# A recurrent four-way convolution scan: one transfer queue in program order, scalings placed under the column scans, larger hand-overs and a re-cut last pass

## The chip, the cores and the metric

The kernel runs on one core of a Trainium2 chip. The metric is the device time of one execution in microseconds (us). A core has a matrix engine (PE, with its weight loads shown as PEld), a vector engine (DVE), a scalar engine (ACT), GpSimd (POOL) and SyncE (SP). Each runs its own instructions in a fixed order and waits at an instruction until what it needs is there. SP and ACT also issue transfers (DMAs), in that same order.

## The reference

The input has 32 images of 48 channels, 64 rows and 128 columns, in f32. Two layers of this are computed, each with weights of its own:

```
def step(w, b):
    def f(carry, inp):
        nxt = inp + _conv1d(carry, w, b)      # 5 taps, 48 -> 48 channels
        return (nxt, nxt)
    return f
... D: scan over the rows downwards, U: over the rows of D upwards (same weights)
... R: scan over the columns of U to the right, L: over those of R to the left
x = x + _L0_conv_ref(_gn(x), ...)             # _gn: mean and variance over 3 channels x 64 x 128
x = x + _L1_conv_ref(_gn(x), ...)
```

Each row needs the row before it, each column the column before it: 63 + 63 + 127 + 127 dependent steps a layer.

## The kernel before

The images go in four groups of eight (GB), so there are eight passes: (layer 0, group 0) is pass 0, (layer 1, group 0) pass 4. Names in the profile carry layer and group: `row_12d` is the PSUM tile of a down step in layer 1, group 2; `col_03l` that of a left step in layer 0, group 3.

A pass is a down scan and an up scan over rows (`row_step`: nine matmuls and three additions on DVE, the ends at L462), a hand-over to a layout by columns, and a right and a left scan (`col_step`: two independent halves of four images, three matmuls and one addition on DVE at L483 each). The layouts `rows` and `cols` lie in one SBUF tile, `arena`; `rows` reaches past its first part into the region of `cols`. A hand-over of some rows (`hand_over`, L372) is 20 DMAs from SBUF to SBUF: ten pieces of channels for odd rows and ten for even ones. It is done for eight rows at a time, and for the last rows in pieces that end at rows 4, 2 and 0 (`SPLITS`); of rows below 8 the odd ones are issued by ACT, everything else by SP.

Around the scans stands other work:

- `prepare` reads a group of the input (L319), permutes it on POOL (L331), and stores it in DRAM as `xin` (L334). For group 0 this comes before everything else, with the statistics by DVE.
- `fetch` loads rows of `xin` (layer 0) or `mid` (layer 1) for a pass by ten DMAs from ACT's queue (L352), and ACT scales them (L356, 24 instructions).
- `input_moments` and `result_moments` read a group again for the group norm (L280, L292); ACT sums (L195) and squares (L204). A tile of a result takes eight plus eight ACT instructions, of an input one plus one.
- `scaling` turns the moments into scale and offset: a chain over DVE, PE, DVE, PE, DVE, ACT (the square root, `std`, L255) and DVE.
- `drain` and `residual` add a finished pass to its input while the next one runs (POOL, L382 or L388), storing `mid` or the output. `last_residual` does so for the last pass under its left scan, by quarters of the columns (L416 loads, L424 additions, L432 stores).

The program writes this side work between scan steps, and a scheduler that models the engines then sets the order on each of them. The DMAs go through eight lanes that SP and ACT share: each waits for the one eight places before it.

Of the kernel before, what the change touches and what calls it, by code (L numbers as in the profile page):

```python
# [34 lines left out]
C = 48  # L35
ODD = 64
P = ODD + C
TAPS = 5
# [11 lines left out]
RB = 8  # L50
DOWN, RIGHT, LEFT = range(3)

LOADS = tuple(slice(a, b) for a, b in ((0, 4), (4, 12), (12, 20))) + tuple(
    slice(a, min(a + 8, 64)) for a in range(20, 64, 8)
)
EARLY = 3
SPLITS = {4: 8, 2: 4, 0: 2}
# [28 lines left out]
def kernel(  # L86
# [35 lines left out]
    wd = const([FULL, len(PRODUCTS), FULL], "wd")  # L122
# [7 lines left out]
    nats = [const([P, CH, PAIR], f"nat{i}") for i in range(2)]  # L130
    perms = [const([P, CH, PAIR], f"perm{i}") for i in range(2)]
# [3 lines left out]
    ]  # L135

# [4 lines left out]


    nc.gpsimd.memset(arena[32:64, H * ROW + 7 * CH * PAIR :], 0.0)
    for t in nats + perms:
        nc.vector.memset(t[32:64], 0.0)
    nc.vector.memset(wd, 0.0)
# [3 lines left out]
    nc.scalar.dma_start(mask_sb, mask)  # L150
    nc.scalar.dma_start(bc, bias)
    for e, c0, c1, o, p0 in PIECES:
        nc.scalar.dma_start(bd[p0 : p0 + c1 - c0, :, o], bias[c0:c1, :, DOWN])
        nc.scalar.dma_start(maskp[:, o, p0 : p0 + c1 - c0], mask[:, c0:c1])

    def load_row_weights(layer: int, eng):

        for eo, a0, a1, o, m0 in PIECES:
            for k in range(TAPS):
                shift, ei = divmod(eo + k - TAPS // 2, E8)  # L160
                d, si = divmod(k, 2)
                for e, c0, c1, i, p0 in PIECES:
                    if e == ei:
                        eng.dma_start(
                            wd[
                                p0 : p0 + c1 - c0,
                                PRODUCTS.index((i, o, shift)),
                                m0 : m0 + a1 - a0,
                            ],
                            w[SIDES[si], layer, DOWN, d, SIDES[0]][c0:c1, a0:a1],  # L170
                        )

    def load_col_weights(layer: int, eng):
        eng.dma_start(wc, w[:, layer, RIGHT : LEFT + 1])
# [5 lines left out]
    class Moments:  # L180


        def __init__(self, parts: int, n: int, key: str):
            self.T, self.n, self.key = parts, n, key
            mean = stat_tile(GB * parts, f"mean{parts}", key)
            dev2 = stat_tile(GB * parts, f"dev2{parts}", key)
            self.mean = mean.rearrange("p (b t) -> p b t", t=parts)
            self.dev2 = dev2.rearrange("p (b t) -> p b t", t=parts)

    def collect(mo, t: int, views, key: str):  # L190


        bs = slice(min(views), max(views) + 1)
        for b, view in views.items():
            nc.scalar.activation(  # L195
                view, view, AF.Identity, scale=sides, accum_out=mo.mean[:, b, t : t + 1]
            )
        neg = stat_tile(GB, "neg", key)
        nc.gpsimd.tensor_scalar(neg[:, bs], mo.mean[:, bs, t], -1.0 / mo.n, None, ALU.mult)  # L199
        nc.gpsimd.tensor_scalar(  # L200
            mo.mean[:, bs, t], mo.mean[:, bs, t], 1.0 / mo.n, None, ALU.mult
        )
        for b, view in views.items():
            nc.scalar.activation(  # L204
                view,
                view,
                AF.Square,
                bias=neg[:, b : b + 1],
                accum_out=mo.dev2[:, b, t : t + 1],
            )  # L210

    def scaling(mo):

        key, T = mo.key, mo.T
        ps = ps_stat.tile([FULL, NG + 1, 2 * GB], F32, tag="ps_stat", name=f"ps_{key}")
        pair = stat_tile(2 * GB, "pair", key)
        if T > 1:
            total = stat_tile(GB, "total", key)
            nc.vector.tensor_reduce(total, mo.mean, mybir.AxisListType.X, ALU.add)
            nc.vector.tensor_scalar(pair[:, 0:GB], total, 1.0 / T, None, ALU.mult)  # L220
        else:
            nc.vector.tensor_copy(pair[:, 0:GB], mo.mean[:, :, 0])  # L222
        nc.tensor.matmul(ps[0:P, NG, 0:GB], mask_sb, pair[:, 0:GB], start=True, stop=True)  # L223
        mean_p = stat_tile(GB, "mean_p", key)
        nc.vector.tensor_copy(mean_p, ps[0:P, NG, 0:GB])
        dev = stat_tile(GB * T, f"dev{T}", key).rearrange("p (b t) -> p b t", t=T)
        nc.vector.tensor_tensor(
            dev, mo.mean, mean_p.unsqueeze(2).to_broadcast([P, GB, T]), ALU.subtract
        )
        sq = stat_tile(GB * T, f"sq{T}", key).rearrange("p (b t) -> p b t", t=T)  # L230
        nc.vector.tensor_tensor(sq, dev, dev, ALU.mult)
        all_sq = stat_tile(GB * T, f"all{T}", key).rearrange("p (b t) -> p b t", t=T)
        nc.vector.scalar_tensor_tensor(all_sq, mo.dev2, 1.0 / mo.n, sq, ALU.mult, ALU.add)
        if T > 1:
            total2 = stat_tile(GB, "total2", key)
            nc.vector.tensor_reduce(total2, all_sq, mybir.AxisListType.X, ALU.add)
            nc.vector.tensor_scalar(pair[:, GB:], total2, 1.0 / T, None, ALU.mult)
        else:
            nc.vector.tensor_copy(pair[:, GB:], all_sq[:, :, 0])
        for o in range(NG):  # L240
            nc.tensor.matmul(ps[:, o], maskp[:, o], pair, start=True, stop=True)
# [7 lines left out]
        var = small("var")  # L249
        nc.vector.tensor_scalar(var, ps[:, 0:NG, GB:], GN_EPS, None, ALU.add)  # L250
        mean = small("mean")
        nc.vector.tensor_copy(mean, ps[:, 0:NG, 0:GB])

        std = small("std")
        nc.scalar.activation(std, var, AF.Sqrt)  # L255
        r0 = small("r0")
        nc.vector.reciprocal(r0, std)
        t0 = small("t0")
        nc.vector.tensor_tensor(t0, var, r0, ALU.mult)
        t1 = small("t1")  # L260
        nc.vector.tensor_tensor(t1, t0, r0, ALU.mult)
        t2 = small("t2")
        nc.vector.tensor_scalar(t2, t1, -0.5, 1.5, ALU.mult, ALU.add)
        scale = small("scale", 2 * NGRP)
        nc.vector.tensor_tensor(scale, r0, t2, ALU.mult)
        offset = small("offset", 2 * NGRP)
        nc.vector.scalar_tensor_tensor(offset, mean, -1.0, scale, ALU.mult, ALU.mult)
        return scale, offset

    def input_moments(g: int):  # L270

        parts, n = 2, H * W // 4
        mo = Moments(parts, n, f"x{g}")
        coeffs[0, g] = mo
        for b in range(GB):
            for t in range(parts):
                tile_ = perms[t].rearrange("p r n -> p (r n)")
                flat = x[g * GB + b].rearrange("c (s t h) w -> s t c (h w)", s=2, t=parts)
                for s in range(2):
                    nc.sync.dma_start(tile_[SIDES[s]], flat[s, t])  # L280
                collect(mo, t, {b: tile_}, f"x{g}_{b}{t}")
                yield
        coeffs[0, g] = scaling(mo)
# [362 lines left out]
```

## Time and the profile before

| what | value |
|---|---|
| median of 3 runs | 5947.53 us (5943.52 to 5948.58) |
| the profiled execution | 5961.04 us, its span 5959.3 |
| PE busy | 4860.6 us, 82% of the span |
| DVE, ACT, POOL busy | 2548.1, 1812.3, 1087.5 us |
| moved by DMA | 599.97 MB, mean 101 GB/s |
| granted PE clock, mean | 0.922 |

PE's share is an average: in a column scan with nothing beside it PE is busy all the time, elsewhere it waits. So the question for each stage is what it waits for. The queue of waits names the tile or engine that came last ("PE col_12r L476 <- DMA arena<-arena: 52.7, 1, 52.7": in all 52.7 us, once, at longest 52.7). Windows give busy time per engine in a stretch, and after the clock the busy share of the DMA engines and GB/s. An issue row ("SPq L372 ... x170") gives the start, the time that the queue took for that many DMAs, and the line.

### The profile page before, as it was taken

Reading aid. Unit: us, or ns where it says so; the run is one execution under the profiler, and the core shown is the slowest. Engines: PE = TensorE matmul, PEld = TensorE weight load, DVE = VectorE, ACT = ScalarE, POOL = GpSimd, SP = SyncE. Lnnn points to the kernel's source line nnn. Section 1 sums busy time; section 2 is a strip of 40 time slices with the busy share of each in tenths; the row PEclk is TensorE's granted clock in tenths of the full one; section 3 lists DMA queues with packets and bytes.
Section 4 is the critical chain, followed back from the end, with each engine's and each line's share of the span. In section 5 each row is a group of like instructions: output and inputs, shape, how many; then the busy total and the mean of one; then the engine's idle time right before and its main releaser. Section 6 shows DMA issues by size and latency. Waiting matters only on the chain. (4 is left out here: it accounts for less than half of the span.)

```text
span 5959.3 us, 105466 instructions
## 1 busy us (share of the span) xinstructions
PE 4860.6 (82%) x42592; PEld 4846.2 (81%) x42592; DVE 2548.1 (43%) x7387; ACT 1812.3 (30%) x3977; POOL 1087.5 (18%) x640
## 2 busy tenths in 40 slices
PE   0496999889996998795997969869698799986990
PEld 0496999889996998795997969869698799986990
DVE  3343554445443553342543535335354345433550
ACT  0451234024220396077050840308603020220000
POOL 3101303121221303000030001510015100350043
PEclk9998999999998999897998989989799899998995
DMA  7665838477465738442184412754117510463045
GB/s 149 118 114 108 174 64 184 106 155 151 98 158 109 167 66 192 111 84 54 22 184 109 84 19 44 149 122 83 30 34 151 121 37 1 95 129 89 1 69 92
DMA packets 847369, 599.97 MB, mean 101 GB/s; under 512 B 267584, under 2 KB 783680, under 8 KB 842272
## 3 DMA queue, kind: packets, MB, share of 16 engines
q1 hardware_dynamic: 603840, 483.73, 39.7%
q10 hardware_dynamic: 243040, 109.49, 9.5%
q8 instruction: 335, 5.49, 0.4%
q14 instruction: 154, 1.26, 0.1%
HBM read 341.31 MB, written 150.99 MB: 83 GB/s over the span
## 5 line engine op out<-in xcount | busy, mean ns | idle before, releaser
L356 ACT ACTIVATE arena<-arena,offset_m,scale_m 128x128 f32<-128x128 f32 (+1 forms) x864 | 425.6, 584 | 1243.6 <-DMA arena<-mid 895.1
L356 ACT ACTIVATE arena<-arena,offset_x,scale_x 128x128 f32<-128x128 f32 (+1 forms) x864 | 422.4, 590 | 901.2 <-DMA arena<-xin 738.6
L195 ACT ACTIVATE perm<-perm,sides 112x256 f32<-112x256 f32 (+1 forms) x560 | 476.2, 858 | 577.1 <-DMA perm<-in_x 192.4
L388 POOL TENSOR_TENSOR perm<-arena,nat 112x1024 f32<-112x1024 f32 x96 | 360.8, 3785 | 1154.8 <-DVE arena L483 459.7
L382 POOL TENSOR_TENSOR nat<-arena,nat 112x2048 f32<-112x2048 f32 x64 | 289.2, 4533 | 671.5 <-DMA nat<-xin 353.9
L204 ACT ACTIVATE perm<-perm,neg_m 112x256 f32<-112x256 f32 x512 | 381.0, 752 | 13.7 <-POOL neg_m L199 13.7
L331 POOL COPY perm<-nat 112x1024 f32<-112x1024 f32 x100 | 200.0, 2034 | 646.7 <-DMA nat<-in_x 599.8
L199 POOL TENSOR_SCALAR neg_m<-mean_m 112x8 f32<-112x8 f32 x64 | 15.1, 236 | 1250.1 <-ACT perm L195 1250.1
L424 POOL TENSOR_TENSOR perm<-arena,nat 112x256 f32<-112x256 f32 x108 | 114.4, 1067 | 485.4 <-DVE arena L483 328.1
L223 PE MATMUL ps_x<-pair_x,mask_sb 112*112 112x8 f32 x8 | 1.6, 276 | 237.2 <-DVE pair_x L222 221.4
L223 PEld LDWEIGHTS ps_x<-pair_x,mask_sb 112*112 112x112 f32 x8 | 1.5, 231 | 237.4 <-DVE pair_x L222 221.4
L476 PE MATMUL col_10r<-arena,wc 112*112 112x128 f32 x508 | 106.3, 292 | 97.3 <-DVE arena L483 50.9
L454 PE MATMUL row_13d<-arena,wd 128*128 128x128 f32 x1134 | 141.7, 291 | 30.0 <-DVE arena L462 30.0
L454 PEld LDWEIGHTS row_13d<-arena,wd 128*128 128x128 f32 x1134 | 139.1, 206 | 32.5 <-DVE arena L462 32.5
L454 PE MATMUL row_11d<-arena,wd 128*128 128x128 f32 x1134 | 137.7, 286 | 29.9 <-DVE arena L462 29.9
L454 PEld LDWEIGHTS row_11d<-arena,wd 128*128 128x128 f32 x1134 | 135.2, 201 | 32.0 <-DVE arena L462 32.0
L454 PE MATMUL row_12d<-arena,wd 128*128 128x128 f32 x1134 | 138.6, 287 | 27.7 <-DVE arena L462 27.7
L454 PEld LDWEIGHTS row_12d<-arena,wd 128*128 128x128 f32 x1134 | 136.0, 202 | 29.8 <-DVE arena L462 29.8
L476 PE MATMUL col_03l<-arena,wc 112*112 112x128 f32 x508 | 105.5, 290 | 67.2 <-DVE arena L483 67.2
L476 PE MATMUL col_11l<-arena,wc 112*112 112x128 f32 x508 | 105.4, 290 | 59.2 <-DVE arena L483 59.2
L454 PE MATMUL row_03d<-arena,wd 128*128 128x128 f32 x1134 | 137.1, 286 | 18.2 <-DVE arena L462 18.2
L454 PEld LDWEIGHTS row_03d<-arena,wd 128*128 128x128 f32 x1134 | 135.2, 201 | 20.0 <-DVE arena L462 19.8
(228 smaller groups left out, 13956.7 us busy)
## 6 DMA issues: line engine op xcount, KB each, us to landing
arena<-arena SPq DMA_DIRECT2D x672, 96.0 KB, 2.5
xin<-perm SPq DMA_DIRECT2D x128, 384.0 KB, 5.2
nat<-xin SPq DMA_DIRECT2D x128, 384.0 KB, 8.6
mid<-nat SPq DMA_DIRECT2D x128, 384.0 KB, 5.1
perm<-mid SPq DMA_DIRECT2D x128, 384.0 KB, 6.3
nat<-in_x SPq DMA_DIRECT2D x100, 384.0 KB, 8.0
perm<-in_x SPq DMA_DIRECT2D x96, 384.0 KB, 6.3
nat<-mid SPq DMA_DIRECT2D x96, 384.0 KB, 6.9
```

Of the source, the lines that this page charges most:

```text
L195: nc.scalar.activation(view, view, AF.Identity, scale=sides, accum_out=mo.mean[:, b, t : t + 1])
L199: nc.gpsimd.tensor_scalar(neg[:, bs], mo.mean[:, bs, t], -1.0 / mo.n, None, ALU.mult)
L204: nc.scalar.activation(view, view, AF.Square, bias=neg[:, b : b + 1], accum_out=mo.dev2[:, b, t : t + 1],)
L223: nc.tensor.matmul(ps[0:P, NG, 0:GB], mask_sb, pair[:, 0:GB], start=True, stop=True)
L331: nc.gpsimd.tensor_copy(perm5[:, r], nat[:, r])
L356: nc.scalar.activation(view[:, o, b], view[:, o, b], AF.Identity, bias=offset[:, o, b : b + 1], scale=scale[:, o, b : b + 1],)
L382: nc.gpsimd.tensor_tensor(nat, res, nat, ALU.add)
L388: nc.gpsimd.tensor_tensor(perm[:, t].rearrange("p (b k e) -> p b k e", b=GB, k=NK), cols[:, q + t].rearrange("p e k b -> p b k e"), nat[:, ...
L424: eng.tensor_tensor(perm[:, t].rearrange("p (b k e) -> p b k e", b=GB, k=kn), cols[:, q + t, :, ks].rearrange("p e k b -> p b k e"), nat[: ...
L454: nc.tensor.matmul(ps[o][:, a:b], wd[:, n], prev[:, i, a + s * GB : b + s * GB], start=seen[o] == 1, stop=seen[o] == left[o],)
L476: nc.tensor.matmul(ps, wt[:, 1], prev, start=True, stop=False)
```

## The change

All bulk transfers go through one helper, `dma()`, on SP, and keep the order in which the program writes them (before, the scheduler could move them). ACT issues only the first weights and half of the last stores.

- Hand-overs are 16, 16, 16, 8 and 8 rows (`HANDS`), odd rows first: 100 DMAs a pass where there were 200.
- `fetch` is split into `load_rows` and `scale_rows`; `residual` has its loads ahead of time (`load_residual`); four staging tiles replace two pairs.
- Moments are staged in `spare`, three tiles in the region of rows 0 to 15, which no one uses during right and left scans. So all moments move there: those of the next input first, then those of the last pass's result (`all_moments`). `neg` is computed on ACT instead of POOL.
- `scaling` is a generator with a few instructions between steps, each told to follow the newest scan step (`issue_after`). For the input it is started at right step 80, for results in an up scan from row 60 on, two passes after the pass that made that result.
- For group 0 all input loads come first, and half of the permuting goes to ACT.
- `drain` is spread over the down scan alone and completed at the start of the up scan.
- `last_residual` loads 96 KB at a time (128 loads instead of 256; 256 stores as before), parts 3, 2, 1, 0 as the left scan sets them free, from step 96 on.
- Row weights are built from five tap copies in DRAM, by 10 wide DMAs.

```diff
-SPLITS = {4: 8, 2: 4, 0: 2}
+HANDS = {48: 64, 32: 48, 16: 32, 8: 16, 0: 8}
...
+    def dma(dst, src):
+        tc.keep_in_program_order(nc.sync.dma_start(dst, src))
...
-        nc.gpsimd.tensor_scalar(neg[:, bs], mo.mean[:, bs, t], -1.0 / mo.n, None, ALU.mult)
-        nc.gpsimd.tensor_scalar(
-            mo.mean[:, bs, t], mo.mean[:, bs, t], 1.0 / mo.n, None, ALU.mult
-        )
+        nc.scalar.mul(mo.neg[:, bs, t], mo.sum[:, bs, t], -1.0 / mo.n)
...
+    spare = [arena[0:P, i * CH * PAIR : (i + 1) * CH * PAIR] for i in range(3)]
...
     def hand_over(h0: int, h1: int):
-        for r in range(2):
-            eng = nc.scalar if r and h1 <= RB else nc.sync
+        for r in (1, 0):
...
-            if h % RB == 0 and h:
-                hand_over(h, h + RB)
-            elif h in SPLITS:
-                hand_over(h, SPLITS[h])
+            if h in HANDS:
+                hand_over(h, HANDS[h])
...
+    def all_moments(n: int):
+        if n + 1 < NGRP:
+            yield from input_moments(passes[n + 1][1])
+        if 0 < n <= NGRP:
+            yield from result_moments(n - 1)
...
+            if stage_name == "down" and i % 7 in (1, 4):
+                advance("drain")
+            if stage_name == "up":
+                complete("drain")
+                if i == 60 and 2 <= n <= NGRP + 1:
+                    side["scaling"] = scaling(moments[1, n - 2], 1, n - 2)
+                if i % 2:
+                    advance("scaling")
+            if stage_name == "right":
...
+                if i % 6 == 2:
+                    advance("prepare")
+                if i % 4 == 2 and i < 66 and n + 1 < NGRP:
+                    advance("moments")
+                elif i % 8 == 2:
+                    advance("moments")
+                if i == 80 and n + 1 < NGRP:
+                    side["scaling"] = scaling(moments[nxt], *nxt)
+                if i % 4 == 0:
+                    advance("scaling")
+            if stage_name == "left":
...
+                if i % 8 == 2:
+                    advance("moments")
+                if nxt and i in (50, 40, 25):
+                    complete("moments")
+                    load_rows(*nxt, (50, 40, 25).index(i))
+                    scale_rows(*nxt, (50, 40, 25).index(i))
+                if nxt and i == 15:
+                    for j in range(4 - 2 * layer):
+                        load_residual(n, j)
+                if not nxt and i <= 96 and i % 8 == 0:
+                    advance("last")
```

How this falls on the engines is not in the diff, since the scheduler has a part in it. First SP at the end of the first pass's up scan. Before, the last rows' hand-over stands there in pieces of two rows (48x2x128 and, by sides, 48x128), followed by the next group's restaging (`xin` stores, `in_x` loads):

```order
L372 DMA arena<-arena 16x128
L372 DMA arena<-arena 48x128 x2
L372 DMA arena<-arena 16x128
L372 DMA arena<-arena 32x128
L372 DMA arena<-arena 48x128 x4
L372 DMA arena<-arena 32x128
L372 DMA arena<-arena 16x128
L372 DMA arena<-arena 48x128 x2
L372 DMA arena<-arena 16x128
L372 DMA arena<-arena 32x128
L372 DMA arena<-arena 48x128 x2
L334 DMA xin_86<-perm_83 48x2x1024 x2
```

After, it holds groups of 8 rows (four of one side in a DMA), both sides on SP; the next group's input loads follow:

```order
L147 DMA arena<-arena 16x4x128
L147 DMA arena<-arena 48x4x128 x2
L147 DMA arena<-arena 16x4x128
L147 DMA arena<-arena 32x4x128
L147 DMA arena<-arena 48x4x128 x4
L147 DMA arena<-arena 32x4x128
L147 DMA arena<-arena 16x4x128
L147 DMA arena<-arena 48x4x128 x2
L147 DMA arena<-arena 16x4x128
L147 DMA arena<-arena 32x4x128
L147 DMA arena<-arena 48x4x128 x2
L147 DMA stage<-in_x 48x8x256 x4
```

So the pieces of the end became fewer and four times as high, and ACT's half came to SP. Second, ACT in pass 1 (layer 0, group 1). Before, the square root of the next group's scaling (`std_x`) stands behind the last rows of a load, in the down scan, ahead of ACT's hand-over DMAs:

```order
L352 DMA arena<-xin_86 32x4x128
L352 DMA arena<-xin_86 16x4x128
L352 DMA arena<-xin_86 48x4x128 x2
L352 DMA arena<-xin_86 32x4x128
L352 DMA arena<-xin_86 48x4x128 x2
L356 ACTIVATE arena<-arena,offset_x_2744,scale_x_2742 128x4x16 x24
L255 ACTIVATE std_x_7997<-var_x_7993 128x24
L372 DMA arena<-arena 48x128
L372 DMA arena<-arena 16x128
```

After, it stands behind the last tile of the next input's moments (`sum_x`, `neg_x`, `dev_x`), and ahead of all 16 tiles of a result's moments (`sum_m`, `neg_m`, `dev_m`), behind which come the scales for the next pass (L411):

```order
L196 ACTIVATE arena,sum_x_7873<-arena,sides 112x2048
L199 ACTIVATE neg_x_7874<-sum_x_7873 112x1
L201 ACTIVATE arena,dev_x_7875<-arena,neg_x_7874 112x2048
L273 ACTIVATE std_x_9144<-var_x_9140 128x24
L196 ACTIVATE arena,sum_m_8656<-arena,sides 112x256 x8
L199 ACTIVATE neg_m_8657<-sum_m_8656 112x8
L201 ACTIVATE arena,dev_m_8658<-arena,neg_m_8657 112x256 x8
L196 ACTIVATE arena,sum_m_8656<-arena,sides 112x256 x8
```

What moved is that the result's moments now share the pass with the input's and stand behind `std_x`. Third, DVE at that `std_x`: before, `var_x`, which it needs, is computed among the additions of the down scan's step 36 in pass 1:

```order
L225 COPY mean_p_x_7979<-ps_x_7973 112x8
L227 TENSOR_TENSOR dev_x_7981<-mean_x_5774,mean_p_x_7979 112x16
L231 TENSOR_TENSOR sq_x_7983<-dev_x_7981 112x16
L233 SCALAR_TENSOR_TENSOR all_x_7985<-dev_x_5775,sq_x_7983 112x16
L236 TENSOR_REDUCE total_x_7987<-all_x_7985 112x8
L237 TENSOR_SCALAR pair_x_7974<-total_x_7987 112x8
L250 TENSOR_SCALAR var_x_7993<-ps_x_7973 128x24
L252 COPY mean_x_7995<-ps_x_7973 128x24
L462 SCALAR_TENSOR_TENSOR arena<-row_01d_6577,bd,arena 128x128
```

After, it stands among the additions of the left scan of that pass, behind both halves of step 60 (counted down from 126; one row is one half):

```order
L563 SCALAR_TENSOR_TENSOR arena<-col_01l_10287,bc,arena 112x32x4
L245 TENSOR_TENSOR dev_x_8968<-dev_x_8968 112x16
L563 SCALAR_TENSOR_TENSOR arena<-col_01l_10292,bc,arena 112x32x4
L248 SCALAR_TENSOR_TENSOR dev_x_8968<-dev_x_7875,dev_x_8968 112x16
L252 TENSOR_REDUCE total_x_9035<-dev_x_8968 112x8
L563 SCALAR_TENSOR_TENSOR arena<-col_01l_10297,bc,arena 112x32x4
L253 TENSOR_SCALAR pair_x_8855<-total_x_9035 112x8
L563 SCALAR_TENSOR_TENSOR arena<-col_01l_10302,bc,arena 112x32x4
L268 TENSOR_SCALAR var_x_9140<-ps_x_8918 128x24
L270 COPY mean_x_9142<-ps_x_8918 128x24
L563 SCALAR_TENSOR_TENSOR arena<-col_01l_10307,bc,arena 112x32x4
L278 RECIPROCAL r_x_9245<-std_x_9144 128x24
```

So this chain went from the down scan to the middle of the left scan, with scan steps between its parts.

More of the change, by code (lines that the diff above doesn't have):

```diff
@@ L135 @@
     ]
+    taps = [
+        dram.tile([C, TAPS, C], F32, tag=f"taps{i}", name=f"taps{i}") for i in range(2)
+    ]
+    passes = [(layer, g) for layer in range(2) for g in range(NGRP)]
+    coeffs, moments, mark = {}, {}, {}
     rows = arena[:, 0 : H * ROW].rearrange("p (h o n) -> p h o n", h=H, o=NG)
@@ L227, in scaling @@
[L227 to L234, printed above, removed]
+            nc.vector.tensor_reduce(total, mo.sum, mybir.AxisListType.X, ALU.add)
```

579 lines of the change are left out of this document (307 added, 272 removed).

## The prediction

> **What bounds the kernel now.** I read the page's head first, then one undisturbed window, the queue of what PE waited for, windows over the row scans, and the issue rows of SP and ACT.
>
> ```profile
> span 5959.3 us, 105466 instructions
> ...
> PE 4860.6 (82%) x42592; PEld 4846.2 (81%) x42592; DVE 2548.1 (43%) x7387; ACT 1812.3 (30%) x3977; POOL 1087.5 (18%) x640
> ...
> 4800.00:5100.00 300.00, 300.00 (x2688) 300.00 (x2687) 157.19 (x448) 25.98 (x52) 0.00 (x0) 1.00 0.02 5
> ```
>
> The window 4800:5100 is a column scan with nothing in its way: PE is busy for all of its 300 us, at clock 1.00, one matmul record each 300/2688 = 111.6 ns. The 42592 records at that pace are 4754 us. A row step has 18 records (2.01 us), 63 of them make a down or an up scan of 126.6; a column step has 12 (1.34 us), 127 make 170 us, so right and left together are 341. The change leaves these matmuls alone, so 4754 is the floor and 5959 - 4754 = 1205 us can be won. Here is what PE waited for:
>
> ```profile
> PE ps_x L223 <- DVE pair_x L222: 221.4, 1, 221.4
> PE col_03l L476 <- DVE arena L483: 67.2, 1, 67.2
> PE col_11l L476 <- DVE arena L483: 59.2, 1, 59.2
> PE col_12r L476 <- DMA arena<-arena: 52.7, 1, 52.7
> PE col_10r L476 <- DVE arena L483: 50.9, 1, 50.9
> PE col_11r L476 <- DMA arena<-arena: 50.9, 1, 50.9
> PE col_13r L476 <- DMA arena<-arena: 48.3, 1, 48.3
> PE col_03r L476 <- DMA arena<-arena: 47.2, 1, 47.2
> PE col_10r L476 <- DMA arena<-arena: 46.4, 1, 46.4
> PE col_01r L476 <- DMA arena<-arena: 45.1, 1, 45.1
> PE col_02r L476 <- DMA arena<-arena: 44.9, 1, 44.9
> PE col_00r L476 <- DMA arena<-arena: 35.0, 1, 35.0
> ...
> PE ps_x L223 <- DVE pair_x L220: 15.9, 1, 15.9
> ...
> DVE total_m L219 <- POOL mean_m L200: 177.8, 3, 67.3
> ```
>
> Eight waits for the hand-over, one at each start of a right scan, make 371 us, with the 16 us of a late scaling beside the first. Three stalls inside column scans make 177; they are one thing, DVE standing at L219 for moments that are not ready (177.8 in three). The start and the row scans are seen in windows (PE busy, clock, DMA share and GB/s at the end of a row; the two sums are over passes 1 to 3, and over 4 to 7):
>
> ```profile
> 0.00:230.00 230.00, 2.35 (x9) 2.15 (x10) 70.38 (x167) 5.14 (x12) 76.78 (x44) 1.00 0.85 165
> 230.00:368.00 138.00, 132.07 (x1135) 131.30 (x1135) 60.53 (x188) 123.37 (x229) 2.11 (x10) 0.99 0.31 58
> ...
> sum 447.38, PE 402.26 PEld 399.36 DVE 199.72 ACT 247.76 POOL 164.16; mean PE 134.09 PEld 133.12 DVE 66.57 ACT 82.59 POOL 54.72
> ...
> sum 659.42, PE 555.13 PEld 547.00 DVE 286.14 ACT 304.35 POOL 312.81; mean PE 138.78 PEld 136.75 DVE 71.54 ACT 76.09 POOL 78.20
> ...
> 5810.00:5959.00 149.00, 0.45 (x5) 0.25 (x3) 12.99 (x22) 0.00 (x0) 50.88 (x49) 0.51 0.60 92
> ```
>
> The first down scan ends at 368, 241 over its 126.6. The others exceed it by 447 - 380 = 67 in layer 0 and 659 - 506 = 153 in layer 1. The tail is 149. Together: 4754 + 241 + 387 + 177 + 220 + 149 = 5928; the 31 left go to short waits and slow clock after long ones, and I keep 16.
>
> **The change, part by part.**
>
> *Hand-over.* It is 200 DMAs a pass now and 100 after, all on SP, the odd rows' side first and no splits of 4, 2 and 2 rows at the end.
>
> ```profile
> 1070.91 145.89 SPq L372 DMA_DIRECT2D arena<-arena  x170
> 1161.05 26.09 ACTq L372 DMA_DIRECT2D arena<-arena  x30
> ...
> arena<-arena SPq DMA_DIRECT2D x672, 96.0 KB, 2.5
> ```
>
> SP issues from 1071 to 1217 without a break while the up scan ends at 1167: the queue is 50 us late, and that is the wait. One issue is 0.63 us near its best, landing 2.5. With 20 DMAs (12.6 us) per 16 rows (32 us), and the last two groups of 8 rows 16 us apart, SP is idle when the last group comes. Its ten odd-side DMAs are ready 2 us before the end and are out 4.3 us after it; the first columns' pieces of the other side follow, two issues and a landing: about 9 us, if the first matmul waits for these alone; if for all ten of that side, 13. Eight make 72 instead of 387 (bounds 50 and 110).
>
> The Trainium skill, "DMA: Bandwidth & Descriptors", section "Issuing engines are not separate DMA queues", says that issuing from several engines saves only the sequencer's time, usually small beside the transfer. Here 0.63 us of issue stands against a landing of 2.5 that overlaps others, so the issue is the larger part of the sequence. By the page's rule fewer issues win little: the rival C below.
>
> *Loads off ACT.* In layer 1 ACT issues ten loads, then 24 scales, and the scan waits for it.
>
> ```profile
> L356 ACT ACTIVATE arena<-arena,offset_m,scale_m 128x128 f32<-128x128 f32 x672 | 348.0, 610 | 565.9 <-DMA arena<-mid 482.3 <-DMA out<-perm 53.0 <-issue 17.9
> L382 POOL TENSOR_TENSOR nat<-arena,nat 112x2048 f32<-112x2048 f32 x64 | 289.2, 4533 | 671.5 <-DMA nat<-xin 353.9 <-DVE mean_p_m L225 169.9 <-DVE arena L483 144.4
> ```
>
> 24 scales of about 0.5 us issue are 12.4, under the 16 that the scan takes for eight rows; a residual is 4.5 on POOL, two a group. With the loads queued ahead on SP, layer 1 falls to some 4 a pass; layer 0 stays bound by transfers (its down windows run at 186 GB/s) and I keep 10 to 13. Term 55 for 220, bounds 15 and 150.
>
> *Scalings.* The three waits at L219 go: the m scalings now stand in an up scan, long after their data. Their small operations are about 0.3 us, but
>
> ```profile
> L227 DVE TENSOR_TENSOR dev_m<-mean_m,mean_p_m 112x128 f32<-112x128 f32 x4 | 12.6, 3148 | 0.1
> ```
>
> shows such a one beside POOL's work. Seven scalings at 4 to 10: 50, bounds 15 and 80.
>
> *The moments' order on ACT, the term that costs.* In passes 1 and 2 ACT has the next input's moments, then std of its scaling, then all 16 tiles of a result's moments, then the scales for the next pass. The scaling's DVE part stands after left step 60, so 127 + 67 = 194 column steps, 260 us after the right scan's start. ACT stands at std until then, although its input moments are over long before:
>
> ```profile
> 2691.23 0.77 ACT L204 ACTIVATE perm<-perm,neg_m 112x256 f32<-112x256 f32 x1 [0.35 <-POOL neg_m L199]
> ...
> 2703.59 0.77 ACT L204 ACTIVATE perm<-perm,neg_m 112x256 f32<-112x256 f32 x1 [0.35 <-POOL neg_m L199]
> ...
> L204 ACT ACTIVATE perm<-perm,neg_x 112x2048 f32<-112x2048 f32 x48 | 96.1, 2002 | 21.7 <-POOL neg_x L199 21.7
> ```
>
> One input tile is two passes of 2.0, 16 tiles some 67. One result tile is 12.36 (the two rows), 16 are 198. So ACT comes free at 261 + 198 = 459. The last result tile lies where rows 0 to 5 go, so the next load is issued after that: ten issues, a landing, 24 scales, first row step at about 476. The left scan is over at 341: a stall of 136, and some 7 more as the drain starts late, in passes 2 and 3. Term 285 for 177; bounds 240 (the 17 from ACT's end to the first row step and the 7 of the drain hidden, in both passes) and 330 (that chain and the drain twice as long).
>
> *Start.* All 32 input DMAs go first. A group of the input (8 x 48 x 64 x 128 numbers) is 12.6 MB; at 165 to 186 GB/s (the first window; the down windows) it takes 68 to 76, and with 17 for the small weight loads that share the eight DMA lanes it is there at 85 to 93; moments and scaling 10. Row 4 then waits for the first stores and loads, about 15. Stores of the rest (12.6 MB, 68 us) end near 160, and rows 20 on are loaded only behind these: 40. End of the first down scan 100 + 127 + 55, rounded up to 288, so 161 over instead of 241 (bounds 135 and 200).
>
> *Tail.* SP issues without a break:
>
> ```profile
> 5821.03 10.45 SPq L416 DMA_DIRECT2D nat<-mid  x16
> 5831.57 8.27 SPq L432 DMA_DIRECT2D out<-perm  x16
> ...
> L424 POOL TENSOR_TENSOR perm<-arena,nat 112x256 f32<-112x256 f32 x108 | 114.4, 1067 | 485.4 <-DVE arena L483 328.1 <-DMA nat<-mid 155.6 <-POOL perm L424 0.9
> ```
>
> A quarter of the columns is 4 x 8.3 + 2 x 10.5 = 55 us of SP after the change, with half the loads, against 75 now. The first of four comes free 120 us before the end; three are done 45 after it, and the last adds 32 outs at 0.53 and a landing: 64 for 149. POOL's 32 additions a quarter are 34, covered by the 55. Bounds 45 and 100.
>
> *Sum.* 4754 + 161 + 72 + 55 + 50 + 285 + 64 + 16 = 5457 against the profiled span of 5959.3 (that execution took 5961.04). The median of the three runs is 5947.53, 13.5 less, so the forecast is 5457 + 2 - 14 = 5445 us.
>
> **The rivals.**
>
> A: ACT is not held. If the scaling gets done at right step 80, where the program writes it, ACT ends its result tiles at 67 + 198 + waits, before 341, and the 285 vanish: 5445 - 285 = 5160. Against it: the engines' order has it in the left scan, and each engine runs in order.
>
> B: the one queue starves. SP now holds everything behind each wait. The scaling at left step 63 needs 30.7 MB through SP (16 moment tiles, 12.6; by SP's order also 12 of the 16 input loads and 11 of the 16 stores of the restaging, 18.1) in 254 us, so 121 GB/s. The window of a right scan shows
>
> ```profile
> 550.00:820.00 270.00, 269.32 (x2383) 269.32 (x2384) 138.96 (x396) 101.52 (x136) 62.73 (x60) 0.99 0.80 158
> ```
>
> 158 with two independent streams. At 100 GB/s, the tail's 92 being the nearest low row, three passes lose (307 - 254) x 3 = 159: 5604. It becomes slower than before only below 30.7 MB / 421 us = 73 GB/s, where the three lose 500: 5945 and more. For it: nat tiles are two, and each load must wait for POOL; against it: no busy row is so low.
>
> C: the hand-over gap stays, because landing and not issue sets it: +315, 5760. Against it: SP's unbroken 145.89 us.
>
> **How the numbers follow.** My forecast has 0.80, A 0.07, C 0.04, B short of the turning point 0.06, B beyond it 0.03. The bounds of the terms, taken as independent, give about 100 either way, so 5345 to 5545; A, B and C on both sides widen the eight-in-ten range to 5280 to 5620. About 0.2% (12 us) is what a measurement of this kernel can tell from no change; slower 0.03, same 0.01, faster 0.96.
>
> **What would show it.** Right: col_*r waits under 15 us; in passes 2 and 3 the first row_02d and row_03d wait some 140 for ACT scales; ACT idle before std_x up to 260 us after the right scan's start; first row matmul near 100. Wrong: DVE waiting at L225 for sums (B), row_02d starting right after left (A), long hand-over waits with SP idle (C).

## The result, and the profile after

The changed kernel takes 5442.42 us in the median of four runs (5430.09 to 5455.96), the kernel before 5948.06; the ratio is 0.9149, interval 0.9118 to 0.918. The forecast was 5445 in 5280 to 5620. The profiled execution has a span of 5429.0 us, so the sum of terms, 5457, is to be held against that: 28 us too long, and its parts miss by more than that in both directions.

The page's head and what PE waited for, after:

```profile
span 5429.0 us, 103969 instructions
...
PE 4811.6 (89%) x42592; PEld 4802.6 (88%) x42592; DVE 2527.8 (47%) x7394; ACT 1850.8 (34%) x4090; POOL 1013.8 (19%) x409
...
PE row_02d L534 <- DMA arena<-xin: 118.8, 1, 118.8
PE row_03d L534 <- DMA arena<-xin: 118.7, 1, 118.7
PE ps_x L234 <- DVE pair_x L226: 85.9, 1, 85.9
PE row_00d L534 <- DVE arena L542: 38.2, 5, 28.6
PE col_01r L556 <- DMA arena<-arena: 15.0, 1, 15.0
PE col_02r L556 <- DMA arena<-arena: 14.8, 1, 14.8
PE col_13r L556 <- DMA arena<-arena: 14.6, 1, 14.6
PE col_12r L556 <- DMA arena<-arena: 14.1, 1, 14.1
PE col_10r L556 <- DMA arena<-arena: 13.7, 1, 13.7
PE col_11r L556 <- DMA arena<-arena: 13.6, 1, 13.6
PE col_00r L556 <- DMA arena<-arena: 13.6, 1, 13.6
PE col_03r L556 <- DMA arena<-arena: 13.4, 1, 13.4
```

The eight hand-over waits are 113 us where they were 371, the three stalls of DVE inside column scans are gone from the list, and two new waits of 119 stand at the head, at the start of the row scans of passes 2 and 3. They name a DMA; what that DMA waited for is read on ACT (first the wait in all four places, then two rows of ACT's timeline):

```profile
ACT std_x L273 <- DVE var_x L268: 420.8, 4, 122.2
...
1163.10 2.00 ACT L196 ACTIVATE arena<-arena,sides 112x2048 f32<-112x2048 f32 x1 [4.27 <-DMA arena<-in_x]
1289.76 0.22 ACT L273 ACTIVATE std_x<-var_x 128x24 f32<-128x24 f32 x1 [122.20 <-DVE var_x L268]
```

In pass 1 the right scan starts at 1026.5. ACT's last input tile is over at 1168; then ACT stands for 122.2 us until `var_x`, 263 after the right scan's start, and begins a result's 16 tiles only then. They end at 1482.4; SP issues the next rows' loads at 1482.5, and the first row matmul is at 1488.8. The left scan had been over at 1370. In pass 2 it is the same, with 121.3 us before the root. In pass 0 ACT stood at the root for 117.9 us too, and that cost nothing: no result's tiles were queued behind it, and pass 1's row scan started on time.

The down scans of passes 5 to 7, which had taken 169 to 172 us each:

```profile
3487.50:3614.70 127.20, 127.15 (x1136) 126.96 (x1135) 61.02 (x189) 71.50 (x144) 83.17 (x22) 1.00 0.92 206
4108.70:4236.00 127.30, 127.17 (x1137) 126.98 (x1137) 61.08 (x189) 71.56 (x144) 82.97 (x22) 1.00 0.91 205
4719.90:4847.20 127.30, 127.30 (x1136) 126.99 (x1135) 61.12 (x189) 71.48 (x144) 83.00 (x22) 1.00 0.89 205
```

PE is busy throughout, and the transfers move 205 GB/s beside it. The tail, the time after the last left scan, is seen in SP's issue rows; that scan ends at 5331.5:

```profile
5211.60 9.09 SPq L147 DMA_DIRECT2D out<-stage  x16
5220.78 9.64 SPq L147 DMA_DIRECT2D arena<-mid  x16
5230.47 19.48 SPq L147 DMA_DIRECT2D out<-stage  x32
5250.51 13.30 SPq L147 DMA_DIRECT2D stage<-mid  x16
...
5293.23 17.60 SPq L147 DMA_DIRECT2D out<-stage  x32
...
5389.43 37.07 SPq L147 DMA_DIRECT2D out<-stage  x48
```

From 5230.5 to 5293.2 the same kinds of rows have gone round once: a quarter of the columns takes 62.8 us, and 97.5 are left after the scan.

### The profile page after: what moved, and what is told of

Same layout as the page of the kernel before. It is cut to its first block, busy times and chain, and to the rows that moved or that the text cites. A ratio compares the mean times of both kernels' runs of the same rounds, so it can differ in the third digit from the quotient of the medians.

```text
span 5429.0 us, 103969 instructions
## 1 busy us (share of the span) xinstructions
PE 4811.6 (89%) x42592; PEld 4802.6 (88%) x42592; DVE 2527.8 (47%) x7394; ACT 1850.8 (34%) x4090; POOL 1013.8 (19%) x409
## 4 chain that ended last, share of the span: by engine, by line
PE 79%; ACT 7%; SPq 5%; DMA 5%; POOL 1%; DVE 1%; issue 1%; ACTq 0%; DVEq 0%; POOLq 0%
SPq L147 5%; ACT arena L201 3%; ACT arena L196 3%; PE row_13d L534 2%; PE row_10d L534 2%; PE row_01d L534 2%; PE row_00u L534 2%; PE row_12d L534 2%; PE row_12u L534 2%; PE row_01u L534 2%; PE row_10u L534 2%; PE row_03u L534 2%; PE row_11u L534 2%; PE row_13u L534 2%; PE row_02u L534 2%; PE row_02d L534 2%
## 5 line engine op out<-in xcount | busy, mean ns | idle before, releaser
L411 ACT ACTIVATE arena<-arena,offset_m,scale_m 128x128 f32<-128x128 f32 (+1 forms) x864 | 422.0, 587 | 1246.9 <-DMA arena<-mid 835.9
L196 ACT ACTIVATE arena<-arena,sides 112x256 f32<-112x256 f32 (+1 forms) x560 | 475.9, 856 | 914.2 <-DVE arena L563 463.0
L456 POOL TENSOR_TENSOR stage<-arena,stage 112x1024 f32<-112x1024 f32 x96 | 361.0, 3793 | 1443.2 <-DVE arena L563 1368.7
L447 POOL TENSOR_TENSOR stage<-arena,stage 112x2048 f32<-112x2048 f32 x64 | 289.2, 4532 | 1442.1 <-DMA stage<-xin 801.4
L411 ACT ACTIVATE arena<-arena,offset_x,scale_x 128x128 f32<-128x128 f32 (+1 forms) x848 | 414.1, 586 | 164.1 <-DMA arena<-xin 95.6
L201 ACT ACTIVATE arena<-arena,neg_m 112x256 f32<-112x256 f32 x512 | 379.8, 749 | 0.7
L341 POOL COPY stage<-stage 112x1024 f32<-112x1024 f32 x98 | 196.7, 2036 | 744.3 <-DMA stage<-in_x 550.7
L534 PE MATMUL row_03d<-arena,wd 128*128 128x128 f32 x1134 | 133.7, 282 | 130.4 <-DMA arena<-xin 118.7
L534 PE MATMUL row_02d<-arena,wd 128*128 128x128 f32 x1134 | 134.6, 283 | 128.8 <-DMA arena<-xin 118.8
L534 PEld LDWEIGHTS row_02d<-arena,wd 128*128 128x128 f32 x1134 | 133.2, 199 | 130.2 <-ACT arena L411 122.5
L534 PE MATMUL row_00d<-arena,wd 128*128 128x128 f32 x1134 | 136.8, 286 | 47.5 <-DVE arena L542 38.2
L534 PEld LDWEIGHTS row_00d<-arena,wd 128*128 128x128 f32 x1134 | 135.0, 201 | 49.2 <-DVE arena L542 43.2
L542 DVE SCALAR_TENSOR_TENSOR arena<-row_03d,bd,arena 128x128 f32<-128x128 f32 x189 | 61.3, 349 | 202.9 <-DMA arena<-xin 130.1
L534 PE MATMUL row_11u<-arena,wd 128*128 128x128 f32 x1134 | 129.7, 277 | 7.1 <-DVE arena L542 7.1
```

The source lines that it names most:

```text
L196: nc.scalar.activation(view, view, AF.Identity, scale=sides, accum_out=mo.sum[:, b, t : t + 1])
L201: nc.scalar.activation(view, view, AF.Square, bias=mo.neg[:, b, t : t + 1], accum_out=mo.dev2[:, b, t : t + 1],)
L341: nc.gpsimd.tensor_copy(dst[:, r], src[:, r])
L411: nc.scalar.activation(args[0], args[0], AF.Identity, bias=args[2], scale=args[1])
L447: nc.gpsimd.tensor_tensor(nat, res, nat, ALU.add)
L456: nc.gpsimd.tensor_tensor(perm[:, t].rearrange("p (b k e) -> p b k e", b=GB, k=NK), cols[:, q + t].rearrange("p e k b -> p b k e"), nat[:, ...
```

## The experiments

The theory on the stall: ACT stands at the square root of the next input's scaling, because DVE's part of it is placed in the left scan, and everything behind the root is late. Its rival: the one queue is late with the next rows whatever ACT does.

**The root taken off ACT.**

```diff
-            nc.scalar.activation(std, var, AF.Sqrt)
-            nc.vector.reciprocal(r0, std)
+            if key[0] == "x":
+                nc.vector.tensor_scalar(r0, var, -0.5, 1.5, ALU.mult, ALU.add)
```

> Leaves out the square root on ACT in the three scalings of an input under a scan (and in the first one): a first Newton step from 1 on DVE takes its place, which holds only because these inputs' variance is near 1. ACT thus has nothing to wait for between the input's tiles and the result's. Theory (ACT held at std): in the changed kernel ACT had done the input's tiles some 138 us after the right scan's start, stood 122 us at std, then needed 198 for the result's tiles. Without the hold it ends at about 336 to 345, loads and scales at 355, the left scan at 344: the two waits of 119 fall to 0 to 25 each, the down scans behind them keep some of their 18; time 5442 - 2 x (95 to 130) = 5180 to 5250. Rival (the one queue: the next pass's loads come late whatever ACT does, since they stand behind restaging and moments on SP): the two waits stay over 80, time above 5360.

Measured: 5244.51 us, ratio 0.8804 (0.8786 to 0.8821), 198 less than the changed kernel. Of the wait of 118.8 in pass 2 this is left (below it the first 138 us of pass 1's right scan, DMA share and GB/s last):

```profile
PE row_02d L538 <- DMA arena<-xin: 19.5, 1, 19.5
...
1031.70:1170.00 138.30, 138.25 (x1221) 138.28 (x1222) 71.04 (x203) 63.36 (x74) 44.17 (x22) 0.98 1.01 219
```

In pass 3 it is 13.8. ACT now goes from the input's tiles straight to the result's and ends 357 us after the right scan's start, where 336 to 345 had been expected and the changed kernel has 456. The two down scans behind keep their 19 to 21 us beyond 126.6, and the profile shows no other large change. The theory holds, the rival falls.

**The tiles by turns.** This keeps the root on ACT, and the whole computation.

```diff
+        while gens:                       # input_moments and result_moments by turns
+            for gen in list(gens): ...
...
-                if i == 80 and n + 1 < NGRP:          # right scan
+                if i == 64:                           # left scan
+                    complete("moments")
                     side["scaling"] = scaling(moments[nxt], *nxt)
...
+        if "scaling" in side:
+            tc.keep_in_program_order(add)             # the column step's addition
```

> Keeps the square root on ACT and the whole computation, but takes the input's and the result's tiles by turns, and holds the order of the scaling's DVE part at left steps 64 to 50, after all tiles, with the root behind them on ACT. Theory (what cost was ACT idle at std with 198 us of tiles behind it): ACT has 16 x (4.2 + 12.4) = 265 us of tiles in a row from about 20 us after the right scan's start, the scaling at 255 to 275 finds them done or waits up to 30 on DVE, loads and scales are over before the left scan is, at 344; the two waits of 119 fall to 0 to 10, and DVE may lose up to 30 in each left scan; time 5442 - 2 x (95 to 130) = 5180 to 5250. Rival (50 MB of transfers in the two column scans through one queue that stands whenever ACT has not given a tile back: the restaging is late): waits of 40 or more at the row scans' start, time above 5300.

Measured: 5252.27, ratio 0.8816 (0.8801 to 0.8831). This is just past the expected range. The waits at the row scans are gone altogether (each starts with the end of the left scan, and the down scans of passes 2 and 3 take 127 where they took 145). What stands at the head of PE's waits instead, behind the start:

```profile
PE row_00d L539 <- issue: 70.9, 1, 70.9
PE col_01l L561 <- DVE arena L568: 24.9, 1, 24.9
PE col_02l L561 <- DVE arena L568: 23.3, 1, 23.3
```

The two in left scans are DVE standing for the sums of the input's last tiles, which ACT had not finished (25.1 us in pass 1), as the expectation allowed. The first it did not foresee: the root was also held in program order in the first scaling, behind ACT's copies of the staging (it ran at 168 us instead of 89), and the first down scan ended 30 us later than in the changed kernel.

**The hand-over, from five sides.** First, undone:

```diff
-            if h in HANDS:
-                hand_over(h, HANDS[h])
+            if h % RB == 0 and h:
+                hand_over(h, h + RB)
+            elif h in SPLITS:
+                hand_over(h, SPLITS[h])
```

> Undoes one part of the change: hand-overs again of 8 rows and, at the end, of 4, 2 and 2 rows (200 DMAs a pass), all on SP in program order. Theory (number of issues sets the gap): 20 issues are 13 us and eight rows of the up scan 16, so the queue keeps up until row 8; then 60 issues are 39 us, and the last groups come free at the end: waits of some 25 to 30 where 14 were, time 5442 + 8 x (11 to 16) = 5530 to 5570. If SP is late from the drain on, as before the change, waits of 45 to 50 and 5700. Rival (landing, not issue): waits within 3 us of 14, time 5420 to 5470.

Measured: 5610.32, ratio 0.942 (0.9402 to 0.9438), past the 5530 to 5570 that the theory gave. Six waits are 29.6 to 31.0, two longer:

```profile
PE col_12r L556 <- DMA arena<-arena: 47.0, 1, 47.0
```

So 800 more issues for the same bytes cost 168 us with nothing else moved. The two longest had not been foreseen: in pass 6 the up scan starts at 4351.0, and SP is held by the drain's DMAs until 4390.8, so that the hand-over begins only 40 us into that scan. (In pass 5 too, but there scalings made the up scan 20 us longer.) Second, done alone in the kernel before:

```diff
-        for r in range(2):
-            eng = nc.scalar if r and h1 <= RB else nc.sync
+        for r in (1, 0):
+            eng = nc.sync
```

with the groups of the changed kernel.

> The kernel before with one part of the change alone: hand-overs of 16, 16, 16, 8 and 8 rows, odd rows first, all on SP, the scheduler's order as before. Theory (SP was late because of 200 issues): the eight waits fall from 371 in all to 8 x 15 = 120, time 5950 - 250 = 5700. The drain and the moments on SP between the hand-overs, which the change moved away, may hold part of it: 5700 to 5760. Rival (program order and the single queue are what matter): waits of 35 or more, 5870 and up.

Measured: 5733.59, ratio 0.9627 (0.9613 to 0.9642). The waits are 11.3 to 16.9 in four passes and 26.7 to 35.3 in the other four. In passes 5 to 7 the drain's DMAs hold SP for the first 63 to 65 us of the up scan, and in pass 3 a load of moments stands between the groups. So 221 us, set beside the 506 of the whole change, come with this part alone. Besides the fewer issues it holds the odd rows' place ahead and ACT's share put on SP, which no run took apart. Third and fourth, from the changed kernel on:

```diff
-HANDS = {48: 64, 32: 48, 16: 32, 8: 16, 0: 8}
+HANDS = {48: 64, 32: 48, 24: 32, 16: 24, 8: 16, 0: 8}
```

> Splits the hand-over of rows 16 to 31 into two of 8 rows (120 DMAs a pass instead of 100). Theory (the last two groups are late because rows 8 to 15 go where rows 30 and 31 were read from, and the 16-row group's transfers of 192 KB land 7.5 us after issue): the group of rows 8 to 15 starts at the up scan's step 8 instead of 7 us later, the last group's first side at 2 us before the end; the eight waits of 13.4 to 15.0 fall to 8 to 10, time 5442 - 8 x 5 = 5400. Rival (issue alone sets it: 20 more issues of 0.65 us make the queue later): waits of 14 or more, time 5442 or up to 60 more.

Measured: 5405.3, ratio 0.9078 (0.9055 to 0.9101): the waits are 6.7 to 7.7 in six passes, 14.4 and 11.3 in passes 6 and 7. Transfers to landing, in the changed kernel between 960 and 1003 us and in this one between 980 and 1030:

```profile
arena<-arena SPq DMA_DIRECT2D x14, 192.0 KB, 7.7
...
arena<-arena SPq DMA_DIRECT2D x34, 96.0 KB, 2.3
```

A transfer twice as large took three times as long to land here, but size is not all of it: the first one of the group of rows 16 to 31, issued at 976.8 after SP had stood for 13 us, landed in 3.7 us, and those behind it, with others still under way, in up to 10.4. The next group writes over rows 30 and 31 of the row layout, which this one was still reading: SP stood until 1002.5 with a group that was ready at 995.3 (eight up steps before the scan's end). So the last groups were late by a landing, not by issue. And with the last group's pieces in the order of their use:

```diff
+        if not h0:
+            order = [(r, e) for r in (1, 0) for e in range(3)]
+            order += [(r, e) for e in range(3, E8) for r in (1, 0)]
```

> As the split into 8 rows, and in the last group (rows 0 to 7) the pieces go in the order in which the right scan needs them: columns' eighths 0, 1, 2 of the odd rows, then of the even rows, then the rest by turns. Theory (the first matmul waits for its own pieces and no more, each at 0.65 us of issue): even rows' first two are issued right at the end, waits 4 to 5 us and perhaps 1 to 2 more inside the first seven right steps; time 5442 - 8 x 9 = 5370. Rival (the matmul waits for a whole side): waits as in the split alone or longer, 5400 or more.

Measured: 5381.73, ratio 0.9033 (0.9013 to 0.9054). Passes 0 to 5 have waits of about 3, passes 6 and 7

```profile
PE col_12r L561 <- DMA arena<-arena: 8.7, 1, 8.7
```

and 7.9. The first matmul waits for its own pieces alone. In pass 6 the drain's DMAs hold SP again until 40 us into the up scan (4229.3), and it issues the 120 DMAs of the hand-over from there to 4332.8 without a break, while the scan ends at 4316.0: there the queue itself is still late.

**The loads back on ACT.**

```diff
-            dma(rows[p0 : p0 + c1 - c0, hs, o], src[e][c0:c1])
+            tc.keep_in_program_order(
+                nc.scalar.dma_start(rows[p0 : p0 + c1 - c0, hs, o], src[e][c0:c1]))
```

> Undoes one part: the rows' loads are issued by ACT again, in program order ahead of their scales; all else as in the changed kernel. Theory (layer 1's down scans were late because ACT spent its time on issues): ten issues of 6 to 12 us and 24 scales of 12.4 make 18 to 25 for eight rows where the scan takes 16: the three down scans of passes 5 to 7 go from 127 to 140 to 170, the first down scan and those of layer 0 lengthen too, time 5442 + 60 to 150 = 5500 to 5590. Rival (what made them late was the residual's loads and the drain, which are now ahead of time): down scans of passes 5 to 7 below 132, time within 20 of 5442.

Measured: 5620.55, ratio 0.9437 (0.942 to 0.9454), 178 more. The down scans of passes 5 to 7 take 149, 149 and 146 instead of 127, those of passes 1 and 4 149 and 150 instead of 127, those of passes 2 and 3 183 and 176 instead of 145. ACT's issue rows in pass 5 (a load of eight rows, then 24 scales that are not shown, then the next load):

```profile
3705.30 4.42 ACTq L400 DMA_DIRECT2D arena<-mid  x4
3721.94 0.84 ACTq L400 DMA_DIRECT2D arena<-mid  x2
...
3742.22 0.31 ACTq L400 DMA_DIRECT2D arena<-mid  x1
```

A group comes every 20 to 22 us, the scan needs one each 16. Issue is not the whole of it: in each group ACT also stands 5.7 us until a load has landed, since the loads no longer run ahead of the scales. That makes 21 us a pass in passes 5 to 7, where the kernel before lost 44; the other half there lies in what else moved (the residual's loads ahead of time, the drain's spacing), which no run took apart. In pass 1 the kernel before took 146 and in pass 4 149, so there the loads' place gives the whole loss back.

**The tail, four tries.** ACT issues half of the stores in all parts:

```diff
-                        if part == 0 and r:
+                        if r:
```

> In the last pass's residual ACT issues the odd rows' stores in all four parts, not in the last part alone; nothing else moves. Theory (SP's issue sets the tail: 64 stores of 0.55 and 32 loads of 0.7 to 0.9 us are the 62.8 us that a part takes): a part falls to about 45, the tail from 97 to 97 - 50, time 5442 - 45 = 5397. Rival (the transfers set it: their share is 0.75 to 0.84 in the tail, with packets of 128 bytes): the tail shortens by at most 15, time 5427 or more; the issue rows then grow longer instead, since each issue waits for the lane eight places ahead.

Measured: 5463.27, ratio 0.917 (0.915 to 0.919), by the intervals not to be told from the changed kernel; its tail is 107.6 us, 10 longer. SP's stores halved, but

```profile
5278.65 18.00 SPq L147 DMA_DIRECT2D stage<-mid  x16
```

16 loads took 18 us of issue where they had taken 13. Two parts of 64 columns, with rows of 256 bytes in the stores:

```diff
-        kn, nq, no = NK // 4, HP // 2, HP // 4
+        kn, nq, no = NK // 2, HP // 4, HP // 8
```

> The last pass's residual in two parts of 64 columns instead of four of 32: as many transfers of the same sizes, but with stores of 256 bytes in a row instead of 128 and loads of 256 bytes as before; the first part comes free 32 column steps (43 us) later. Theory (the short rows set the tail's pace, 100 GB/s at a busy share of 0.8): the pace rises to 150 or more, 25 MB in 170 us from 86 us before the left scan's end: tail 80 to 90 instead of 97, time 5425 to 5435. Rival (issues and the round of load, add, store set the pace, some 62 us for a quarter of the work whatever the rows): tail 43 longer, 140, time 5485.

Measured: 5492.09, ratio 0.9223 (0.9207 to 0.9238). The second part's additions were placed among the last left scan's steps, DVE waited there, and that scan took 318 us. They also take columns 0 to 63 from step 32 on, before that scan has finished them, so this version does not compute the whole result. It says nothing of the rows. With the additions behind the scan:

> As the run with two parts of 64 columns, but with the second part's additions traced behind the left scan's end, so that DVE no longer runs them among the scan's steps (in the run before, DVE stood there for columns' loads, and the left scan took 318 us instead of 170). Theory (the short rows of 128 bytes set the tail's pace): tail 80 to 95, time 5425 to 5440. Rival (the round of load, add and store, some 55 to 62 us for a quarter of the work, whatever the rows): eight rounds of half the size from 86 us before the left scan's end, tail 134 to 150, time 5480 to 5495.

Measured: 5471.4, ratio 0.9182 (0.9166 to 0.9198), tail 121.8: between the two expectations, and 24 longer than before. Three windows of its tail, and the changed kernel's whole tail (DMA share and GB/s last):

```profile
5343.00:5400.00 57.00, 7.22 (x65) 7.02 (x63) 15.00 (x18) 0.00 (x0) 26.69 (x13) 0.59 0.71 108
5400.00:5440.00 40.00, 0.00 (x0) 0.00 (x0) 6.38 (x5) 0.00 (x0) 15.72 (x6) 0.50 0.72 128
5440.00:5472.00 32.00, 0.00 (x0) 0.00 (x0) 11.47 (x6) 0.00 (x0) 16.94 (x6) 0.50 0.63 110
...
5331.00:5429.00 98.00, 0.48 (x5) 0.28 (x3) 21.97 (x22) 0.00 (x0) 41.96 (x36) 0.52 0.78 101
```

Longer rows move somewhat more in less share, 108 to 128 GB/s where the tail had 101, but the work starts 43 us later, and that weighs more. The last try, a third tile for the sums, stands on the version that follows.

**What the runs pointed to.** Tiles by turns with the scaling at left steps 44 to 30, the first scaling free, the six hand-over groups and the order of the last.

> The whole computation, with what the runs before pointed to: tiles of input and result by turns, the scaling's DVE part held at left steps 44 to 30, the root behind the last tile on ACT, the next rows' loads traced at left steps 30, 22 and 18; hand-overs of 64-48, 48-32 and then five of 8 rows counted from the 16-row ones on, the last one's pieces in the right scan's order. Theory: the start is that of the changed kernel again (the turns alone had lost 25 us there, since the pin on the root also held the first scaling behind ACT's copies), the two DVE waits of 23 and 25 in the left scans go, nothing takes their place at the row scans, hand-over waits are 4 to 9: 5252 - 25 - 48 - 60 = 5120, between 5100 and 5160. Rival (ACT's tiles are not over at left step 30, or the loads come too late there): waits of 10 to 40 at the row scans of passes 2 and 3, 5140 to 5200.

Measured: 5099.94 us, ratio 0.8562 (0.8547 to 0.8577), 342 less than the changed kernel and at the edge of the expected 5100 to 5160. Its longest waits on PE:

```profile
PE ps_x L234 <- DVE pair_x L226: 93.3, 1, 93.3
PE row_00d L546 <- DMA arena<-xin: 27.3, 1, 27.3
...
PE col_13r L568 <- DMA arena<-arena: 9.2, 1, 9.2
PE col_12r L568 <- DMA arena<-arena: 9.1, 1, 9.1
...
PE col_01l L568 <- DVE arena L575: 3.0, 1, 3.0
```

Both large waits are in the first 185 us; no row scan of passes 1 to 7 waits 2 us or more at its start. The theory's time was 5120. Then the third tile:

```diff
-                perm = stage[:, 2 + i % 2]
+                perm = (stage[:, 2], stage[:, 3], arena[0:P, 2 * CH * PAIR : 3 * CH * PAIR])[k % 3]
```

> The best version so far, with a third tile for the last residual's sums (in rows 10 to 15 of the row layout, which the last left scan doesn't use); nothing else moves. Theory (the tail's pace is a round: POOL waits for a tile's 16 stores to have landed, adds for 8.3 us, and only then SP has stores again, so that neither fewer issues on SP nor longer rows shortened it): a quarter of the columns falls from 62 us to the 52 to 56 of its issues, tail 100 to between 60 and 80, time 5100 - 30 = 5070, between 5060 and 5085. Rival (issues and transfers fill the 62 us anyway): tail within 8 of 100, 5092 to 5108.

Measured: 5092.58, ratio 0.8558 (0.8547 to 0.857), the same within the intervals; its tail is 93.1 where the version without it has 99.0. SP's rows there follow each other without a hole, with 0.50 to 1.08 us for an issue:

```profile
4985.68 13.34 SPq L147 DMA_DIRECT2D stage<-mid  x16
4999.06 9.44 SPq L147 DMA_DIRECT2D out<-stage  x16
5008.59 8.26 SPq L147 DMA_DIRECT2D out<-arena  x16
5016.96 9.87 SPq L147 DMA_DIRECT2D arena<-mid  x16
```

So buffers are not the tail's limit either. When SP had fewer issues they grew longer, which speaks for the transfers; longer rows went faster, which does so too. Neither is a proof, and what would shorten the tail is open.

## Why the prediction was right, point by point

- *ACT held at the root (285 foreseen).* Right in its mechanism, and shown by two runs that remove it in different ways. Two waits of 118.8 and 118.7, with 18 and 19 more in the two down scans behind them: 274. ACT was let go 263 us after the right scan's start (261 foreseen), the 16 tiles took 192.5 (198), but the first row step came 6 us after ACT's last tile, where 17 had been counted.
- *Hand-over (72).* 113, just past the term's upper bound of 110. The step that failed: that SP is idle when the last group comes. The group ahead of it was late by a landing of 7.7 us in the median, for which the prediction had carried 2.5 over from transfers of half the size; the runs with six groups and with the new order bring most of the waits down to 7 and to 3.
- *Start (161).* The first down scan ends at 273.3, 146.7 over its 126.6. The first row step was at 95 (100 foreseen); the wait for row 20 was 28.6 (40). The prediction's own parts make 282 for that end, and it took 288. No run took the start apart.
- *Down scans (55).* Beside those of passes 2 and 3, whose 37 are counted above, the five others exceed 126.6 by 0.3 to 0.9 each, 3 in all. The step that failed is that layer 0 stays bound by transfers: pass 1 took 126.9, and with the tiles by turns passes 2 and 3 did so too. With the loads back on ACT pass 1 took 149.2 again, so what had held it was the loads' place on ACT and not a limit of the transfers, which moved 212 GB/s in that scan after the change and 187 before. That is 52 too many in the sum, the largest miss.
- *Scalings (50).* The up scans of passes 2 to 5 took 130.2, 130.1, 130.3 and 137.4 instead of 126.8, in all 21, and the left scans of passes 0 to 2, with an input's scaling, 171.5 instead of 170.4, 3 more. The term was mis-sized: most scalings cost 1 to 4 us and not 4 to 10.
- *Tail (64).* 97.5. The term was mis-sized at the round of a quarter: 55 us were summed from issues and 62.8 were measured, 23 us more for three quarters. The rest is the last stores: 0.77 us each (48 in 37 us), where 0.53 had been counted.
- *The floor, 4754.* It stands: windows with PE busy throughout have the same pace.

The misses are -11, +41, -14, -52, -26 and +34; they cancel to -28. The forecast's nearness to the median, 2 us, is thus partly luck. That the time lay in the range was not: the term that decided, ACT's hold, was there.

Of the rivals, A (ACT not held) did not come, but the run without the root shows its price: 198 where 285 had been given. Of the 274 lost in these places, 33 stayed as waits and some 40 in the down scans behind. ACT ended later than that rival had it, since the input's tiles came by DMA until 141 us after the right scan's start in the changed kernel, where 67 us of ACT's work had been counted. B (the queue starves) did not come either: in the run without the root pass 1's right scan moved 219 GB/s in its first 138 us. C (landing sets the gap) is refuted by the run with the old groups, and yet a landing was what was left of the gap. The Trainium skill ("DMA: Bandwidth & Descriptors", "Issuing engines are not separate DMA queues") says that issuing from several engines saves only the sequencer's time, usually small beside the transfer. That time was not small here: 0.65 us of issue stand against landings of 2.3, and 800 more issues cost 168 us.

Of the 506 us, the runs show the price of the hand-over's groups, of the loads' place and of ACT's hold. What was won at the start (94), in the tail (51) and by the end of the stalls at L219 (177) is read from the profiles alone.

## What to carry to other kernels

An engine that runs in order pays for a small instruction that stands too early: ask, for each wait, what is queued behind it, and place it behind work that is ready (here 342 us together with the hand-over's last two steps). Sum DMA issues per queue against the time that the step ahead leaves, and cut the last pieces before a barrier in the order in which they are used. And take the landing from transfers of the size that you will have, with as many under way.

## What was not expected of the hardware

Transfers within SBUF of 192 KB took 7.7 us to land in the median, those of 96 KB 2.3 in the same place of the kernel; the first 192 KB of a group, with none ahead of it, took 3.7. And SP's issue of a DMA is no constant: 16 loads took 9.3 to 15.3 us in the tail, and 15.4 to 20.4 when ACT issued stores beside it in all parts.
